# A local-attention convolution with whitening: first loads in smaller parts, one row point in other PSUM banks, one softmax later, half of the last products on quarters of the array

## The chip, the cores and the metric

The kernel runs on one core of a Trainium2 chip. The core has TensorE (PE, matrix products, with its weight loads shown as PEld), VectorE (DVE), ScalarE (ACT), GpSimd (POOL) and SyncE (SP), which each run their own queue of instructions in order, and 16 DMA engines. SP and POOL issue the DMAs. The metric is device microseconds of one execution; for the kernel before there are eight runs, and one execution that was profiled.

## The reference

What is computed, cut to what matters (B = 4 images, C = 256 channels, 64 x 64 pixels, 7 x 7 taps with dilation 2):

```python
k = conv(x, w1, 7x7, dilation 2, 256 -> 128 channels) + b1
k = conv(k, w2, 1x1, 128 -> 49) + b2
attn = softmax(k, axis=1)                       # 49 weights for each pixel
shifts = the 49 shifted copies of x (7 x 7, dilation 2)
y = einsum('bkchw,bkhw->bchw', shifts, attn)
# whitening of y, in 4 groups of 64 channels:
Sigma = 1e-5 * I + cov(y)                       # 64 x 64 for each group
P = five Newton steps to Sigma_N ** -0.5
out = (P * sqrt(1/trace)) @ (y - mean) * weight + bias
```

All data are fp32.

## The kernel before, in words

Rows and columns of an image are split by parity, since the dilation is 2. A "slot" holds the even or the odd rows of one image: 128 partitions (channels) x 2 halves of the channels (NCC = 2) x 32 rows x 64 columns. slots[2b + pr] is row parity pr of image b.

The two convolutions are first folded to one: at lines 181 to 226, w1 is loaded (four DMAs: the first 64 input channels of both halves, then the other 64), multiplied by w2 on PE in chunks of CB = 10 channels (line 210, into the two conv banks cv0 and cv1 in turn), evicted to tapT by ACT and DVE in turn, transposed in fours (line 228) and evicted to tap. Behind w1, the same SP queue loads slots 0 and 1 (load_x, line 129).

The 7 x 7 convolution is computed by a Toom-Cook scheme with seven points for rows and columns (EVAL, points 0, 1, -1, 2, -2, 1/2 and infinity). For a row point br, row_weights, weights, row_eval and col_eval make transformed weights wr and transformed images xh on DVE and ACT (helpers add, sub, madd at lines 289 to 296 record all of these); conv_bank (line 491) does the products for three banks of column points, BANKS = ((1, 2, 0), (3, 4, 6), (5,)), into cv0 and cv1 in turn; pv takes the result; col_interp and row_interp go back to logits. Points that are done directly in the column direction use direct (line 597): 56 passes of some 480 columns each. For image 0 the row points 4, 5 (the point 1/2), 0 and infinity are direct, and their sums go to acc, a PSUM tile of two banks, or to a conv bank. PE writes fp32 products in two passes, and the two row parities go to two column halves of the array (output partitions 0 to 48 and 64 to 112).

From line 690 or so to line 745 the order of image 0 is written out by hand (strict order on DVE): banks, row_weights, keep_weights, row_eval, direct0, col_interp, row_interp, prepare. The lines that the change touches are:

```python
    row_weights(5)
    keep_weights(5)
    col_interp(0, 2)
    ...
    row_eval(0, 5, [rb[0], rb[1], xrs[5]])
    direct0(4, 1)
    col_interp(0, 3)
```

For images 1 to 3 a loop over steps runs conv_step(k, i), i = 0, 1, 2 for the three banks of row point k. Between them a plan puts the softmax of the image before (soft(b, pc) for column parity pc: transposes at line 783, maxima on DVE at 789 and 792, exponentials on ACT at 797, normalisation on DVE at 801 to 810) and its gather: the weights go through zt (line 843), a DRAM buffer sd and 12 DMAs to band, which DVE transposes (line 894); PE turns x into blocks (912, evicted to xb at 920), sums with band (941, to y) and the result y is put back into the slot (960), turned again (973, 981) and added to the second moments sig (994). Image 1's steps begin with bank 0, bank 1, soft(0, 0), bank 2, the infinity product of the image (inf), soft(0, 1).

At the end the whitening matrices are made (whiten, lines 1172 to 1246; a generator for each half of the channels). Pm is 128 x 128 and block-diagonal with two 64 x 64 blocks. The last loop multiplies each 128 x 512 piece of the slots by Pm (line 1262), scales and shifts it on ACT (1273) or DVE (1277) in turn into a tile out (four buffers), and stores 512 KB for each pair of row parities (1281): 64 products, 32 stores.

Of the kernel before, what the change touches and what calls it, by code (L numbers as in the profile page):

```python
# [31 lines left out]
def kernel(  # L32
# [69 lines left out]
    def tp():  # L102
        return ps_tp.tile([P, 512], F32, tag="tp", name="tp")
# [74 lines left out]
    tapT = w1p.tile([P, KT, P], F32, name="tapT")  # L178


    for c0 in range(0, P, P // 2):
        for cc in range(NCC):
            nc.sync.dma_start(
                w1_sb[cc][:, c0 : c0 + P // 2].rearrange("o c t -> o (c t)"),
                w1[:, cc * P + c0 : cc * P + c0 + P // 2].rearrange("o c u v -> o (c u v)"),
            )
    load_x(0, 0, nc.sync)
    load_x(1, 1, nc.sync)
    for cc in range(NCC):
        cs = slice(cc * P, (cc + 1) * P)  # L190
        nc.sync.dma_start(gain_sb[:, cc : cc + 1], gain[0, cs].rearrange("c a b -> c (a b)"))
# [9 lines left out]
    def evict(k, o, i):  # L201
        (nc.vector.tensor_copy if k % 2 else nc.scalar.copy)(o, i)

    CB = 10
    for k, c0 in enumerate(range(0, P, CB)):
        n = min(CB, P - c0)
        t = cv_buf[k % 2]
# [463 lines left out]
    def direct0(br, sr):  # L671
        if br in kept:
            gb = gb5 if br == 5 else gbr
            direct(0, br, sr, acc[:, sr], [gb[:, v, :, sr] for v in range(KS)], xrs[br])
        else:
            u = KS - 1 - 4 * sr - (3 if br == INF else 0)
            w = [tap[:, UPOS[u], v] for v in range(KS)]
            direct(0, br, sr, conv_psum() if br == INF else acc[:, sr], w)
# [41 lines left out]
    bank(2, 2)  # L720
    row_weights(5)
    keep_weights(5)
    col_interp(0, 2)

    for sr in range(2):
        nc.scalar.copy(
# [4 lines left out]
        "p (q r c w) -> p q r c w", q=Q8, r=2, c=NCC  # L731
    )
    row_eval(0, 5, [rb[0], rb[1], xrs[5]])
    direct0(4, 1)
    col_interp(0, 3)
    row_interp(0, 0)
# [417 lines left out]
    nc.gpsimd.memset(blk, 0.0)  # L1154
    for g in range(P // GW):
# [10 lines left out]
    def square(name):  # L1166
        return bpool.tile([P, P], F32, tag="xb", name=name, bufs=4)

    wm, sc, beta = {}, {}, {}

    def whiten(cc):


        def evict(o, i):
            (nc.vector.tensor_copy if cc else nc.scalar.copy)(o, i)

        G = sig[:, cc]
        mu = work.tile([P, 1], F32, tag="mu", name=f"mu{cc}")
        nc.vector.tensor_scalar(mu, G[:, GW : GW + 1], 1.0 / NPIX, None, ALU.mult)
        D = square(f"D{cc}")  # L1180
        nc.vector.tensor_scalar(D, ident, mu, None, ALU.mult)
# [25 lines left out]


        i15 = square(f"i15_{cc}")
        nc.vector.tensor_scalar(i15, ident, 1.5, None, ALU.mult)  # L1210
        Pm = PS[:, 0]
        nc.vector.scalar_tensor_tensor(Pm, S, -0.5, i15, ALU.mult, ALU.add)
        yield

        for it in range(1, T_ITERS):
            t = tp()
            nc.tensor.matmul(
                t[:, : 2 * P], Pm, PS.rearrange("p a c -> p (a c)"), start=True, stop=True
            )
# [16 lines left out]
        scale = work.tile([P, 1], F32, tag="scale", name=f"scale{cc}")  # L1236
# [6 lines left out]
        bt = work.tile([P, 1], F32, tag="beta", name=f"beta{cc}")  # L1243
        nc.vector.tensor_scalar(bt, t[:, :1], scale, -1.0, ALU.mult, ALU.mult)
        nc.vector.tensor_tensor(bt, bt, shift_sb[:, cc : cc + 1], ALU.add)
        wm[cc], sc[cc], beta[cc] = Pm, scale, bt

    chains = [whiten(cc) for cc in range(NCC)]
    for _ in itertools.zip_longest(*chains):
        pass  # L1250


    NT = 512
    TR = NT // W
    n = 0
    for b in (3, 2, 1, 0):
        for cc in range(NCC):
            for q in range(SH // TR):
                st = rpool.tile([P, TR, 2, W], F32, tag="out", name=f"out_{b}_{cc}_{q}", bufs=4)
                for pr in range(2):  # L1260
                    t = tp()
                    nc.tensor.matmul(  # L1262
                        t,
                        wm[cc],
                        slots[2 * b + pr][:, cc, q * TR : (q + 1) * TR, :].rearrange(
                            "p r w -> p (r w)"
                        ),
                        start=True,
                        stop=True,
                    )  # L1270
                    t3 = t.rearrange("p (r w) -> p r w", w=W)
                    if n % 2 == 0:
                        nc.scalar.activation(  # L1273
                            st[:, :, pr, :], t3, AF.Identity, bias=beta[cc], scale=sc[cc]
                        )
                    else:
                        nc.vector.tensor_scalar(  # L1277
                            st[:, :, pr, :], t3, sc[cc], beta[cc], ALU.mult, ALU.add
                        )
                    n += 1  # L1280
                nc.sync.dma_start(
                    out[b, cc * P : (cc + 1) * P, 2 * q * TR : 2 * (q + 1) * TR, :],
                    st.rearrange("p r two w -> p (r two) w"),
                )


# [29 lines left out]
```

## Time and profile before

| | |
|---|---|
| median of 8 runs | 771.3 us (770.2 to 773.13) |
| the profiled execution | 770.2 us |
| its span, first to last instruction | 768.4 us |
| mean granted TensorE clock | 0.986 |

Busy time by stage, in us, from the windows of the profiled execution:

| stage | window | length | PE | DVE | ACT | DMA share |
|---|---|---|---|---|---|---|
| w1 folded, transposed | 0 to 33 | 33.0 | 21.8 | 11.6 | 8.1 | 0.98 |
| first direct products of image 0 | 33 to 58.3 | 25.3 | 23.5 | 24.4 | 6.0 | 0.85 |
| rest of image 0 | 58.3 to 172.1 | 113.8 | 105.5 | 106.4 | 30.7 | 0.15 |
| start of image 1, first softmax | 172.1 to 202.5 | 30.4 | 27.9 | 28.4 | 17.1 | 0.58 |
| images 1 to 3 with the gather of the one before | 202.5 to 604 | 401.5 | 385.1 | 368.8 | 197.8 | 0.43 |
| gather of the last image | 604 to 694 | 90.0 | 84.4 | 47.5 | 40.0 | 0.45 |
| whitening matrices | 694 to 708.5 | 14.5 | 11.3 | 10.4 | 2.6 | 0.01 |
| last products and stores | 708.5 to 768.4 | 59.9 | 55.2 | 26.3 | 24.9 | 0.69 |

How to read what follows: a line of the order of time gives start, duration, engine, line of the kernel, operation, the tile written and the tiles read, its shapes and how many instructions were merged; in square brackets stands how long the engine had been idle and which engine's result ended it. A line of the groups gives busy time in us and the mean of one instruction in ns behind the bar. A line of the windows gives for each engine the busy time and the number of instructions, then the granted clock, the DMA share and GB/s. An fp32 matmul shows as two passes. In the chain of work that ended last, PE has 40% of the span, DVE 33%, ACT 7%.

### The profile page before, as it was taken

The page shows a single profiled execution, that of the slowest core. Times are in us where ns is not written, and L with a number is a line of the kernel's source. Part 1 is how long each engine was busy: PE and PEld are TensorE (multiplying, and loading weights), DVE is VectorE, ACT ScalarE, POOL GpSimd, SP SyncE. Part 2 cuts the span into 40 slices and gives each one's busy share as a digit, 9 for nine tenths or more (in the row PEclk, how much of TensorE's full clock was granted, in tenths as well). Part 3 has the DMA queues.
Part 4 walks back from the last instruction along what each step waited for, and adds up shares of the span by engine and source line. Part 5 has one row for each costly group of instructions (what it writes and reads, how often), then busy time and mean ns, then how long its engine had stood idle before and what let it go on. Part 6 is the DMA issues. An engine that isn't in the chain of part 4 may idle for free.

```text
span 768.4 us, 18362 instructions
## 1 busy us (share of the span) xinstructions
PE 714.6 (93%) x7444; PEld 542.8 (71%) x7444; DVE 623.7 (81%) x1302; ACT 327.1 (43%) x950; POOL 34.2 (4%) x46
## 2 busy tenths in 40 slices
PE   4899997999999999989999999998999889998997
PEld 1349553265888886879988957898998678885443
DVE  2698999999999999979996999699979766535443
ACT  1413241035644653466445434725435663322443
POOL 0230000030000010001000100000000000000000
PEclk9999999899999999989999999999999999999999
DMA  8991110033554582055634820533422143380776
GB/s 332 241 303 62 44 74 37 0 139 124 161 164 146 193 297 68 21 192 186 226 113 167 287 68 2 165 102 107 162 71 85 44 144 115 106 326 25 288 307 280
DMA packets 58717, 114.76 MB, mean 149 GB/s; under 512 B 22615, under 2 KB 41736, under 8 KB 57352
## 3 DMA queue, kind: packets, MB, share of 16 engines
q1 hardware_dynamic: 54936, 94.71, 36.7%
q0 software_dynamic: 3696, 18.88, 7.3%
q8 instruction: 59, 0.97, 0.5%
q14 instruction: 26, 0.21, 0.1%
HBM read 66.23 MB, written 47.33 MB: 148 GB/s over the span
## 4 chain that ended last, share of the span: by engine, by line
PE 40%; DVE 33%; ACT 7%; issue 4%; DMA 3%; SPq 1%; DVEq 0%; ACTq 0%
PE y L941 12%; PE cv L491 12%; PE tp L1262 7%; DVE xh L296 4%; DVE pv L296 3%; PE tp L973 3%; PE tp L912 3%; PE sig L994 3%; DVE zz L296 3%; DVE band L894 2%; DVE ct L296 2%; DVE pv L292 2%; DVE ct L289 2%; ACT zt L843 2%; DVE rb L296 2%
## 5 line engine op out<-in xcount | busy, mean ns | idle before, releaser
L491 PE MATMUL cv<-xh,wr 128*49 128x128 f32 x4368 | 250.5, 275 | 0.0
L491 PEld LDWEIGHTS cv<-xh,wr 128*49 128x49 f32 x4368 | 244.2, 124 | 5.0 <-issue 2.5
L941 PE MATMUL y<-band,xb 128*128 128x224 f32 (+2 forms) x640 | 152.0, 377 | 12.0 <-ACT xb L920 10.3
L941 PEld LDWEIGHTS y<-band,xb 128*128 128x128 f32 x640 | 110.2, 194 | 33.6 <-ACT xb L920 12.8
L960 ACT ACTIVATE slot<-y,pivot 128x512 f32<-128x512 f32 x53 | 36.8, 741 | 60.5 <-PE y L941 60.5
L981 ACT COPY yt<-tp 128x256 f32<-128x256 f32 x128 | 45.5, 378 | 34.9 <-PE tp L973 33.8
L501 ACT COPY pv<-cv 113x486 f32<-113x486 f32 (+1 forms) x63 | 29.8, 475 | 68.4 <-PE cv L491 67.2
L912 PE MATMUL tp<-ident,slot 128*128 128x128 f32 x256 | 50.0, 297 | 7.4 <-ACT yt L981 7.4
L973 PE MATMUL tp<-ident,slot 128*128 128x128 f32 x256 | 51.8, 298 | 4.2 <-ACT xb L920 1.7
L894 DVE STREAM_TRANSPOSE band<-band 128x960 f32<-128x960 f32 (+1 forms) x48 | 51.0, 1063 | 2.8 <-DMA band<-sd 2.7
L973 PEld LDWEIGHTS tp<-ident,slot 128*128 128x128 f32 x256 | 41.3, 205 | 14.2 <-issue 4.5
L912 PEld LDWEIGHTS tp<-ident,slot 128*128 128x128 f32 x256 | 39.9, 205 | 14.3 <-ACT yt L981 9.3
L1277 DVE TENSOR_SCALAR out<-tp,scale,beta 128x512 f32<-128x512 f32 x32 | 25.9, 810 | 29.5 <-PE tp L1262 29.5
L843 ACT COPY zt<-d 32x112 f32<-32x112 f32 (+2 forms) x156 | 45.0, 288 | 1.7
L797 ACT ACTIVATE d<-tp,mx 128x49 f32<-128x49 f32 x128 | 37.0, 338 | 14.4 <-DVE mx L792 14.4
L1273 ACT ACTIVATE out<-tp,beta,scale 128x512 f32<-128x512 f32 x32 | 24.9, 778 | 32.0 <-PE tp L1262 32.0
L296 DVE SCALAR_TENSOR_TENSOR xh<-ct 128x512 f32<-128x512 f32 x42 | 28.0, 693 | 12.3 <-PE cv L491 12.1
L994 PEld LDWEIGHTS sig<-yt 128*64 128x64 f32 x1024 | 32.4, 137 | 6.3 <-issue 4.7
L994 PE MATMUL sig<-yt 128*64 128x65 f32 x1024 | 36.9, 225 | 0.0
L1262 PE MATMUL tp<-slot,PS 128*128 128x512 f32 x80 | 35.9, 593 | 0.0
L920 ACT COPY xb<-tp 128x256 f32<-128x256 f32 x87 | 30.5, 377 | 12.2 <-PE tp L912 11.5
L296 DVE SCALAR_TENSOR_TENSOR pv<-pv 113x162 f32<-113x162 f32 x105 | 34.3, 327 | 1.0
(203 smaller groups left out, 994.8 us busy)
## 6 DMA issues: line engine op xcount, KB each, us to landing
out_dram<-out SPq DMA_DIRECT2D x32, 512.0 KB, 2.6
sd<-zt SPq DMA_DIRECT2D x16, 896.0 KB, 3.9
slot<-in_x_dram POOLq DMA_DIRECT2D x12, 1024.0 KB, 9.4
band<-sd SPq DMA_DIRECT2D x128, 84.0 KB, 2.1
wr<-gd SPq DMA_DIRECT2D x15, 588.0 KB, 4.3
wr<-gd SPq DMA_DIRECT2D x15, 490.0 KB, 3.6
w<-in_L_conv_w_dram SPq DMA_DIRECT2D x4, 1568.0 KB, 11.9
spill<-slot POOLq DMA_DIRECT2D x3, 2048.0 KB, 7.5
```

What stands on the lines that cost most here:

```text
L296: return in_turn(STT(o, a, f, b, ALU.mult, ALU.add))
L491: nc.tensor.matmul(cv[h * HB : h * HB + KT, k, sr : sr + n, sc : sc + n], wv[:, sc, sr, cc], xh[bc][:, :n, h * NCC + cc, :n], start=(j == ...
L797: nc.scalar.activation(d[:, h, i], lt[i // NI][:, i % NI, h, :KT], AF.Exp, bias=mx[:, i, h : h + 1], accum_out=s[:, h, i : i + 1],)
L843: ins = nc.scalar.copy(o, i)
L894: nc.vector.transpose(f, f)
L912: nc.tensor.transpose(t[:, cc * P : (cc + 1) * P], xt[:, cc, CR * m : CR * (m + 1), bass.ds(pc, SW, 2)], ident,)
L941: nc.tensor.matmul(ps[:, cc, q0 - half * HALF : q1 - half * HALF, :], xb[:, cc * P : (cc + 1) * P], rhs, start=(k == 0), stop=(k == len(PI ...
L960: last = nc.scalar.activation(o, ps[:, cc], AF.Identity, bias=pivot[:, cc : cc + 1])
L973: nc.tensor.transpose(t[:, cc * P : (cc + 1) * P], yt[:, cc, CR * i : CR * (i + 1), bass.ds(pc, SW, 2)], ident,)
L981: nc.scalar.copy(yb.rearrange("p a g c -> p (a g) c")[:, :, :GW], t[:, :C].rearrange("p (e c) -> p e c", c=GW),)
L994: nc.tensor.matmul(sig[g * GW : (g + 1) * GW, cc], yb[:, cc, g, :GW], yb[:, cc, g], start=(count[0] == 0 and cc == 0), stop=(count[0] == 4 ...
L1262: nc.tensor.matmul(t, wm[cc], slots[2 * b + pr][:, cc, q * TR : (q + 1) * TR, :].rearrange("p r w -> p (r w)"), start=True, stop=True,)
```

## The change

Five edits in one:

- The load of w1 comes in five parts of 30, 30, 30, 20 and 18 input channels for both halves (ten DMAs instead of four). The parts end where the chunks of ten end.
- Slots 0 and 1 are loaded by row phases: the rows 4q + a of both slots and both halves for a = 3, then 0, 1, 2 (16 DMAs of 256 KB instead of four of 1 MB).
- The direct products of row point 5 (1/2) of image 0 go to the conv banks instead of acc, and row_eval(0, 5) stands before col_interp(0, 2).
- In image 1, soft(0, 0) stands behind the third bank's step instead of before it.
- In the last loop a group is two pieces of both row parities. The even rows are multiplied as before (two 128 x 128 products). The odd rows of the two pieces are multiplied by the two 64 x 64 blocks of Pm in four products, each on a quarter of the array: for the first piece, channels 0 to 63 go to output partitions 0 to 63 and 64 to 127 to 64 to 127; for the second piece the outputs are exchanged, so that the four products use the four pairs of row half and column half. They go to two PSUM banks, y's and the conv banks in turn. The exchanged piece is evicted in two instructions of 64 partitions, with scale and shift for the exchanged partitions, abx, which a product with an exchange matrix swap makes at the end of whiten. The tile out has six buffers.

```diff
-    for c0 in range(0, P, P // 2):
+    CB = 10
+    for c0, c1 in ((0, 3), (3, 6), (6, 9), (9, 11), (11, 13)):
+        c0, c1 = c0 * CB, min(c1 * CB, P)
         for cc in range(NCC):
             nc.sync.dma_start(
-                w1_sb[cc][:, c0 : c0 + P // 2].rearrange("o c t -> o (c t)"),
+                w1_sb[cc][:, c0:c1].rearrange("o c t -> o (c t)"),
...
-    load_x(0, 0, nc.sync)
-    load_x(1, 1, nc.sync)
+    for pr in range(2):
+        slots[pr] = store[pr]
+    for a in (3, 0, 1, 2):
+        for pr in range(2):
+            for cc in range(NCC):
+                nc.sync.dma_start(
+                    store[pr][:, cc].rearrange("c (q a) w -> c a q w", a=4)[:, a],
+                    x[0, cc * P : (cc + 1) * P].rearrange(
+                        "c (q a two) w -> c two a q w", two=2, a=4
+                    )[:, pr, a],
+                )
...
-            direct(0, br, sr, acc[:, sr], [gb[:, v, :, sr] for v in range(KS)], xrs[br])
+            direct(
+                0, br, sr, conv_psum() if br == 5 else acc[:, sr],
+                [gb[:, v, :, sr] for v in range(KS)], xrs[br],
+            )
...
-    col_interp(0, 2)
...
     row_eval(0, 5, [rb[0], rb[1], xrs[5]])
+    col_interp(0, 2)
     direct0(4, 1)
...
-                *steps[:2], (0, lambda: soft(0, 0)), steps[2], inf, (0, lambda: soft(0, 1)),
+                *steps[:3], (0, lambda: soft(0, 0)), inf, (0, lambda: soft(0, 1)),
...
+    swap = rpool.tile([P, P], F32, name="swap")
+    for g in range(P // GW):
+        nc.gpsimd.tensor_copy(
+            swap[:, g * GW : (g + 1) * GW], ident[:, (1 - g) * GW : (2 - g) * GW]
+        )
...
+        t = tp()
+        nc.tensor.matmul(t[:, :2], swap, ab, start=True, stop=True)
+        abx[cc] = work.tile([P, 2], F32, tag="abx", name=f"abx{cc}")
+        nc.vector.tensor_copy(abx[cc], t[:, :2])
...
+                def plain(k):
+                    t = tp()
+                    pe(nc.tensor.matmul(t, wm[cc], y[0][k], start=True, stop=True))
+                    out_rows(st[k][:, :, 0, :], rows_of(t), sc[cc], beta[cc])
...
+                plain(0)
+                for k in range(2):
+                    for i in (G0, G1):
+                        o = i if k == 0 else (G1 if i is G0 else G0)
+                        pe(
+                            nc.tensor.matmul(
+                                ts[k][o], wm[cc][i, i], y[1][k][i],
+                                start=True, stop=True, skip_group_check=True,
+                            )
+                        )
+                out_rows(st[0][:, :, 1, :], rows_of(ts[0]), sc[cc], beta[cc])
+                store(0)
+                for i, o in ((G1, G0), (G0, G1)):
+                    out_rows(
+                        st[1][o][:, :, 1, :], rows_of(ts[1])[i], abx[cc][i, 0:1], abx[cc][i, 1:2]
+                    )
+                plain(1)
+                store(1)
```

out_rows is the scaling and shifting on ACT and DVE in turn; store is the DMA of 512 KB.

More of the change, by code (lines that the diff above doesn't have):

```diff
@@ L178 @@
     tapT = w1p.tile([P, KT, P], F32, name="tapT")
-    for c0 in range(0, P, P // 2):
+    CB = 10
+    for c0, c1 in ((0, 3), (3, 6), (6, 9), (9, 11), (11, 13)):
+        c0, c1 = c0 * CB, min(c1 * CB, P)
         for cc in range(NCC):
             nc.sync.dma_start(
-                w1_sb[cc][:, c0 : c0 + P // 2].rearrange("o c t -> o (c t)"),
-                w1[:, cc * P + c0 : cc * P + c0 + P // 2].rearrange("o c u v -> o (c u v)"),
-            )
-    load_x(0, 0, nc.sync)
-    load_x(1, 1, nc.sync)
+                w1_sb[cc][:, c0:c1].rearrange("o c t -> o (c t)"),
+                w1[:, cc * P + c0 : cc * P + c1].rearrange("o c u v -> o (c u v)"),
+            )
+    for pr in range(2):
[9 more added lines that the diff above has]
+                )
     for cc in range(NCC):
@@ L202, in evict @@
         (nc.vector.tensor_copy if k % 2 else nc.scalar.copy)(o, i)
-    CB = 10
     for k, c0 in enumerate(range(0, P, CB)):
@@ L1167, in square @@
         return bpool.tile([P, P], F32, tag="xb", name=name, bufs=4)
-    wm, sc, beta = {}, {}, {}
+    wm, sc, beta, abx = {}, {}, {}, {}
     def whiten(cc):
@@ L1235, in whiten @@
         nc.vector.scalar_tensor_tensor(q, qi, rtr, q, ALU.mult, ALU.add)
-        scale = work.tile([P, 1], F32, tag="scale", name=f"scale{cc}")
+        ab = work.tile([P, 2], F32, tag="ab", name=f"ab{cc}")
+        scale = ab[:, 0:1]
         nc.vector.scalar_tensor_tensor(
@@ L1242, in whiten @@
         yield
-        bt = work.tile([P, 1], F32, tag="beta", name=f"beta{cc}")
+        bt = ab[:, 1:2]
         nc.vector.tensor_scalar(bt, t[:, :1], scale, -1.0, ALU.mult, ALU.mult)
@@ L1246, in whiten @@
         wm[cc], sc[cc], beta[cc] = Pm, scale, bt
+        yield
+        t = tp()
+        nc.tensor.matmul(t[:, :2], swap, ab, start=True, stop=True)
+        abx[cc] = work.tile([P, 2], F32, tag="abx", name=f"abx{cc}")
+        nc.vector.tensor_copy(abx[cc], t[:, :2])
     chains = [whiten(cc) for cc in range(NCC)]
@@ L1254, with out_rows, two_banks @@
     TR = NT // W
-    n = 0
+    n = [0]
+    def out_rows(o, i, scale, bias):
+        n[0] += 1
+        if n[0] % 2:
+            nc.scalar.activation(o, i, AF.Identity, bias=bias, scale=scale)
+        else:
+            nc.vector.tensor_scalar(o, i, scale, bias, ALU.mult, ALU.add)
+    def two_banks():
+        while True:
+            t = ps_y.tile([P, 2, NT], F32, tag="y", name="apply")
+            yield [t[:, k] for k in range(2)]
+            yield cv_buf
+    G0, G1 = slice(0, GW), slice(GW, P)
@@ L1256 @@
+    two = two_banks()
     for b in (3, 2, 1, 0):
         for cc in range(NCC):
-            for q in range(SH // TR):
-                st = rpool.tile([P, TR, 2, W], F32, tag="out", name=f"out_{b}_{cc}_{q}", bufs=4)
-                for pr in range(2):
-                    t = tp()
[L1262 to L1269, printed above, removed]
-                    )
[L1271 to L1274, printed above, removed]
-                        )
[L1276 to L1284, printed above, removed]
@@ new lines, with store @@
+            for q in range(0, SH // TR, 2):
+                st = [
+                    rpool.tile([P, TR, 2, W], F32, tag="out", name=f"out_{b}_{cc}_{q + k}", bufs=6)
+                    for k in range(2)
+                ]
+                y = [
+                    [
+                        slots[2 * b + pr][:, cc, (q + k) * TR : (q + k + 1) * TR, :].rearrange(
+                            "p r w -> p (r w)"
+                        )
+                        for k in range(2)
+                    ]
+                    for pr in range(2)
+                ]
+                rows_of = lambda t: t.rearrange("p (r w) -> p r w", w=W)
+                ts = next(two)
+                def plain(k):
+                    t = tp()
+                    pe(nc.tensor.matmul(t, wm[cc], y[0][k], start=True, stop=True))
+                    out_rows(st[k][:, :, 0, :], rows_of(t), sc[cc], beta[cc])
+                def store(k):
+                    nc.sync.dma_start(
+                        out[
+                            b, cc * P : (cc + 1) * P, 2 * (q + k) * TR : 2 * (q + k + 1) * TR, :
+                        ],
+                        st[k].rearrange("p r two w -> p (r two) w"),
+                    )
+                plain(0)
[7 more added lines that the diff above has]
+                            )
+                        )
+                out_rows(st[0][:, :, 1, :], rows_of(ts[0]), sc[cc], beta[cc])
[6 more added lines that the diff above has]
+                store(1)
```

## The prediction

> **What bounds the kernel now.** I read the share of busy time first, then the busy time by stage, then the order of time at the places that the change touches, and last the instruction order of both programs, engine by engine. From the page:
>
> ```profile
> PE 714.6 (93%) x7444; PEld 542.8 (71%) x7444; DVE 623.7 (81%) x1302; ACT 327.1 (43%) x950; POOL 34.2 (4%) x46
> L1262 PE MATMUL tp<-slot,PS 128*128 128x512 f32 x80 | 35.9, 593 | 0.0
> L994 PE MATMUL sig<-yt 128*64 128x65 f32 x1024 | 36.9, 225 | 0.0
> ```
>
> The kernel is a chain of stages with different limits, so three places are read on their own. First the head, 0 to 66 us, in order of time:
>
> ```profile
> 9.26 1.87 PE L210 MATMUL cv<-w,w2T 128*49 128x490 f32 x2 [4.54 <-DMA w<-in_L_conv_w_dram]
> 13.03 13.54 PE L210 MATMUL cv<-w,w2T 128*49 128x490 f32 x50 [1.90 <-DMA w<-in_L_conv_w_dram]
> 36.75 9.94 PE L597 MATMUL cv<-slot,tap 128*49 128x512 f32 x48 [1.84 <-DMA slot<-in_x_dram]
> 42.32 4.62 DVE L289 TENSOR_TENSOR rb<-slot 128x1024 f32<-128x1024 f32 x4
> 64.28 0.36 DVE L289 TENSOR_TENSOR wr<-ct 128x196 f32<-128x196 f32 x1 [3.14 <-PE cv L491]
> ```
>
> PE folds w1 only from 13.03, when 64 columns of both halves have landed; it meets the last x load at 36.75; and VectorE, without a gap from 29.66, waits once, for PE's first bank, until 64.28. From there to 172 VectorE is the engine without idle time (106.4 of 113.8 us busy) and the chain of waits runs along it. Second, the turn from image 0 to image 1:
>
> ```profile
> 134.76 14.21 PE L597 MATMUL acc<-slot,gb 128*49 128x512 f32 x56 [4.77 <-DVE zz L289]
> 177.76 0.30 ACT L501 COPY pv<-cv 113x162 f32<-113x162 f32 x1 [4.84 <-PE cv L491]
> 177.96 0.31 ACT L797 ACTIVATE d<-tp,mx 128x49 f32<-128x49 f32 x1
> 202.54 1.34 PE L941 MATMUL y<-band,xb 128*128 128x320 f32 x4 [1.65 <-ACT xb L920]
> ```
>
> PE waits for VectorE at 134.76, but VectorE does not wait for PE there. Third, the tail:
>
> ```profile
> 708.49 27.71 PE L1262 MATMUL tp<-slot,PS 128*128 128x512 f32 x64
> 740.00:750.00 10.00, 10.00 (x25) 4.46 (x24) 4.56 (x7) 4.67 (x6) 0.00 (x0) 1.00 0.74 302
> ```
>
> 128 passes (two for each of 64 fp32 products) stand 0.429 us apart, 55 us without a gap, while ACT and DVE are 46% busy and DMA has a share of 0.74 at 302 GB/s. The tail is PE's alone.
>
> **What the Trainium skill says.** (1) "TensorEngine Tiling (Array Packing)", section Tiling Modes: a 64x64 configuration has four independent tiles, and a change of tiling mode drains TensorE. The trace shows two column halves side by side (line 994: 32 passes of 65 columns in 1.15 us, 36 ns each, where 65 columns alone take 65 x 0.429/512 = 54 ns), never row halves; its drain, from records on both sides of such a change (lines 941 to 994 and 994 to 912), is 0.10 us each way. (2) "TensorE: Matmul & The Clock Gate", Part 3, says of packed tiles that matmuls are "strict FIFO, no reordering". The trace disagrees: at 13.03 two passes for different column halves start 7 ns apart although the first one's second pass stands between them in the program. (3) The same page, Part 1: after an idle window of some 3.4 us PE runs at half rate. The trace agrees: after 4.77 us of idle the 56 passes at 134.76 took 14.21 us, against 11.59 when warm. (4) "DMA: Bandwidth & Descriptors", Specifications, gives about 358 GB/s per core for HBM. The w1 load moved 398 to 452 GB/s, so I take the measured packet: 4096 B in 159 ns, 16 engines, 412 GB/s.
>
> **The change part by part.**
>
> *w1 in five parts.* The same bytes flow: a 12,544 B packet takes 469 ns, and the first half-load (8 packets per engine, 3.75 us) landed at 9.26, so the stream starts at 5.45. Between the two measured packets, a 5,880 B packet should take 224 ns, so both halves of the first 30 columns land at 5.45 + 2 x 8 x 0.224 = 9.1 us, against 13.03. Later parts land at 12.7, 16.3, 18.8 and 21.0; chunks 3, 6, 9 and 11 would want them at 13.4, 16.2, 19.2 and 21.0 if the old rhythm is moved by 3.9. They just fit. The last part of tapT moves from 27.1 to about 23.3: 3.8 us earlier for PE and VectorE. Six more issues on SP at about 0.4 us run ahead of the stream and cost nothing.
>
> *x by row phases.* Still 256 B packets, 4 MB in about 16.3 us (20.4 to 36.7), now four quarters, near 25, 29, 33 and 37 us. The INF product needs only phase 3 and the next only phase 0. Transposes of the weights end at 33.0 - 3.8 = 29.2, so PE no longer meets x: 112 passes at 0.203 us end near 52.1 where they ended at 58.3. PE gains 6 us, of which 2.1 is the stall. VectorE reaches its first use of all phases at 42.3 - 3.8 = 38.5, with x due at 37.3; slots 2 and 3 (POOL's queue, from about 36) collide with the last quarter for up to 1 us. VectorE's wait for the first bank shrinks from 3.14 to about 1 us, so from 64 on it is 3.8 + 2.1 = 5.9 us ahead. A miss of 1 us in x is absorbed by that remaining wait. Taken: -5.9; bounds -3 (slower 256 B reads) and -6.5.
>
> *Row point 1/2.* Both products go to the two conv banks, and row_eval(0, 5) (8.2 us on DVE) comes before col_interp(0, 2) (6.8 us). DVE has the same work in another order, and no wait of its own to lose, so it gains nothing. PE does the two products from 129.9 to 153 instead of 134.8 to 161.2. A new wait comes in: bank 2 of image 1's first point shares cv1 with the second product, and DVE reads that only at 167.8. On PE the third bank and the softmax transposes queue behind it, until about 175.9 on the old clock; DVE comes to those only at 178, so it is covered. Cost 0.
>
> *First softmax behind the third bank.* In the new DVE order the maxima stand behind all four adds of the next row point and their negation behind the 2,048-element add. So: pivot 1.13, four adds 4.7, maxima 0.95, sum 2.2 after 172.09 gives 181.3, and the exponentials start at 181.9 instead of 177.96. zt is filled from 186.9 instead of 183.7 and sd leaves 3.2 us later. On the other side PE does the INF product of image 1 before, DVE loses its waits of 1.27 and 0.73 us, and the first gather matmul was not waiting for the band but for ACT, which was held by col_interp of the first point (copy at 201.44). In the new order I get that copy at 198.2, xb at 201.5 and the first y near 201.6 against 202.54. Sum -0.5, bounds -2.5 and +3.5 (the whole delay of the exponentials arrives). After 260 the orders are the same, so what is gained is carried on.
>
> *Whitening products.* A group is two chunks of both row parities. Before: 8 passes, 8 x 0.429 = 3.43 us. After: 4 plain passes 1.72, four 64x64 products with two passes each, side by side, 2 x 0.429 + 0.02 = 0.88, two mode changes 0.20: 2.80 us. 16 groups: 44.8 for 54.9, -10.1. Evictions are five a group, 5 x 0.8 / 2 = 2.0 us on each engine, under 2.8. Stores are 1.05 MB a group, 2.54 us at 412 GB/s: under 2.8, but 91%. Added before: beta must be complete, then a 128x2 product with swap for each half: first main product at about 709.4 instead of 708.5, +0.9. Two stores now leave close together at the end, +0.4. The tail: -8.8. Its unknown is the four-way overlap; bounds: nothing overlaps more than two (4 passes long, 58.2 us, so +3.3 + 1.3 = +4.6), and full overlap, -9.5. The page (1) and the freedom between the two halves in the trace make me take four. swap's two copies on POOL lie near 601 where POOL is idle.
>
> **The sum.** -5.9 - 0.5 - 8.8 = -15.2 on the profiled span of 768.4 (execution 770.2): 753.2 and 755.0. The runs' median is 771.3, 1.1 above this execution; so 756.1.
>
> **Rivals.**
> - *Two at a time.* If row halves of the array do not run side by side, the four products take four pass times: -6.4 + 4.6 gives 769.5. For it: no row half was ever seen here. Against: the skill's four tiles, and the queues per half seen at 13.03. If three run at once, about 763.
> - *Slower: one tile blocks the queue.* Each fp32 product has two passes on the same tile. If PE begins passes strictly in program order where row halves are involved, each second pass holds the next product back: starts at 0, 1, 1, 2, 2, 3, 3, 4 pass times, so 5 in all. A group then takes 9 passes and 0.2 us: 4.06 x 16 = 65.0, +10.1 + 1.3, less 6.4: 776. It decides from 1.83 us for the four products on (1.72 - 0.20 + 5.05/16), where I expect 0.88. Against it stands the start at 13.03.
> - *The stores become the bound.* At 358 GB/s the 16.8 MB need 46.9 us from the first store at 712: about 758. It only shaves my forecast.
> - *The change does not do what it says at the head*: strided reads make x late and VectorE waits at its row evaluation; then 3 us of the 5.9 are left and the time is 759.
>
> **Chances.** Forecast, with the full stores beside it, 0.76; x late 0.06; two or three at a time 0.11; blocked queue or another loss 0.07. The forecast's own range is 751 to 761; it leaves too much out, so I take 750 to 766, which adds late x and three at once. What a measurement of this kernel can tell from no change is about 0.2%, 1.5 us: two at a time sits on this edge and is split. Faster 0.87, within 0.05, slower 0.08.
>
> **What would show it.** First w1 product with both halves near 9.1; line 597 without a wait on x; DVE's wait for the first bank near 1 us instead of 3.14; the two gb products from about 124 on; exponentials later against the pivot (10 us after it, now 6) yet the first y no later; in the tail a group each 2.8 us, with four passes starting within 30 ns, DMA share about 0.9. A group of 3.6 or 4.1 us proves me wrong, as does a VectorE that waits for x before row_eval by more than 2 us.

## The result, and the profile after

The kernel after took 760.38 us in the median of 11 runs (756.73 to 763.39); the kernel before, in 32 runs beside it and earlier, 772.2 us (768.9 to 774.99). The ratio is 0.985, with a 95% interval of 0.9833 to 0.9867. A second series on another chip gave 761.72 us beside 771.07, ratio 0.9886 (0.9858 to 0.9914). So the change saves 9 to 12 us; 15.2 were forecast. The profiled execution of the kernel after took 763.28 us, its span is 761.5 (before: 768.4).

The busy time, from the page of the kernel after:

```profile
PE 708.4 (93%) x7512; PEld 534.6 (70%) x7512; DVE 630.6 (83%) x1312; ACT 332.4 (44%) x958; POOL 34.4 (5%) x48
```

The shares have hardly moved. The three places have to be read on their own again. The head of the kernel after, in order of time:

```profile
6.87 15.62 PE L221 MATMUL cv<-w,w2T 128*49 128x490 f32 x52 [2.15 <-DMA w<-in_L_conv_w_dram]
...
28.90 11.59 PE L608 MATMUL cv<-slot,tap 128*49 128x512 f32 x56
40.31 11.55 PE L608 MATMUL acc<-slot,tap 128*49 128x512 f32 x56
...
38.22 4.62 DVE L300 TENSOR_TENSOR rb<-slot 128x1024 f32<-128x1024 f32 x4
57.29 0.36 DVE L300 TENSOR_TENSOR wr<-ct 128x196 f32<-128x196 f32 x1 [0.43 <-PE cv L502]
```

PE starts on w1 at 6.87 and does not wait for it again, the direct passes (line 597 before, 608 now) run without a wait for x, and VectorE's wait for the first bank has shrunk from 3.14 to 0.43 us: at this point the kernel is 6.99 us ahead (57.29 for 64.28). VectorE's first instruction behind image 0 (pivot, 165.08 for 172.09) has the same lead. Then the turn to image 1:

```profile
151.35 6.96 PE L502 MATMUL cv<-xh,wr 128*49 128x128 f32 x96 [5.59 <-DVE xh L300]
161.54 7.93 PE L502 MATMUL cv<-xh,wr 128*49 128x128 f32 x112 [3.23 <-DVE zz L300]
169.40 1.22 PE L797 MATMUL tp<-ident,slot 113*128 113x113 f32 x8
...
174.08 0.68 ACT L468 COPY xh<-rb 128x512 f32<-128x512 f32 x1 [4.28 <-DVE rb L300]
174.65 0.31 ACT L811 ACTIVATE d<-tp,mx 128x49 f32<-128x49 f32 x1
...
195.74 1.18 DVE L908 STREAM_TRANSPOSE band<-band 128x960 f32<-128x960 f32 x1 [3.36 <-DMA band<-sd]
197.02 1.31 PE L955 MATMUL y<-band,xb 128*128 128x320 f32 x4 [3.12 <-DMA band<-sd]
```

PE waits twice for VectorE, the softmax transposes come at 169.40, the exponentials start 9.6 us behind the pivot (5.9 before), and now both VectorE and PE wait for the bands. The first y is 5.5 us earlier than before, not 7, and when the whitening matrices begin (the first matmul with blk, 691.98 for 694.87) only 2.9 us of the lead are left. Two single profiles can mislead by some us (a second profile of the old head follows with the tail experiment), but the runs below show that part of the gain was lost here. The tail, in order of time, and two windows of it (busy us and count of PE, PEld, DVE, ACT, POOL, then the granted clock, the DMA share, GB/s):

```profile
706.63 1.40 PE L1324 MATMUL tp<-slot,PS 128*128 128x512 f32 x2
707.96 1.99 PE L1340 MATMUL apply<-slot,PS 64*64 64x512 f32 x8
709.88 2.39 PE L1324 MATMUL tp<-slot,PS 128*128 128x512 f32 x4
...
715.13 1.09 PE L1340 MATMUL apply<-slot,PS 64*64 64x512 f32 x8
716.15 1.98 PE L1324 MATMUL tp<-slot,PS 128*128 128x512 f32 x4
718.07 1.09 PE L1340 MATMUL cv<-slot,PS 64*64 64x512 f32 x8
```

```profile
708.00:710.00 2.00, 2.00 (x10) 0.39 (x9) 0.00 (x0) 0.78 (x1) 0.00 (x0) 0.50 0.00 0
...
734.00:744.00 10.00, 10.00 (x40) 3.08 (x39) 7.04 (x9) 6.27 (x9) 0.00 (x0) 1.00 0.89 365
```

The four products on quarters run side by side: in the trace their second passes start at 715.612, 715.619, 715.625 and 715.632. A group takes 2.93 us (715.13 to 718.07). But the first products stand in a stretch at half clock (707.3 to 710.7), and from the first main product to the end it is 54.9 us where it was 59.9.

### The profile page after: what moved, and what is told of

Its sections match the earlier page's. It is cut to its first block, busy times and chain, and to the rows that moved or that the text cites. A ratio compares the mean times of both kernels' runs of the same rounds, so it can differ in the third digit from the quotient of the medians.

```text
span 761.5 us, 18542 instructions
## 1 busy us (share of the span) xinstructions
PE 708.4 (93%) x7512; PEld 534.6 (70%) x7512; DVE 630.6 (83%) x1312; ACT 332.4 (44%) x958; POOL 34.4 (5%) x48
## 4 chain that ended last, share of the span: by engine, by line
DVE 37%; PE 36%; ACT 7%; issue 4%; DMA 4%; SPq 0%; DVEq 0%; ACTq 0%
PE y L955 11%; PE cv L502 9%; PE tp L1324 4%; DVE xh L307 4%; DVE pv L307 3%; DVE zz L307 3%; PE tp L926 3%; PE sig L1008 3%; PE tp L987 2%; DVE rb L307 2%; DVE ct L300 2%; ACT zt L857 2%; DVE ct L307 2%; DMA band<-sd 2%; DVE rb L300 2%
## 5 line engine op out<-in xcount | busy, mean ns | idle before, releaser
L955 PE MATMUL y<-band,xb 128*128 128x224 f32 (+2 forms) x640 | 153.7, 380 | 13.5 <-ACT xb L934 8.7
L307 DVE SCALAR_TENSOR_TENSOR xh<-ct 128x512 f32<-128x512 f32 x42 | 27.9, 686 | 12.3 <-PE cv L502 12.1
L934 DVE COPY xb<-tp 128x256 f32<-128x256 f32 x41 | 16.5, 422 | 22.2 <-PE tp L926 22.2
L608 PE MATMUL cv<-slot,wi 128*49 128x496 f32 (+3 forms) x168 | 34.8, 571 | 0.0
L811 ACT ACTIVATION_READ_ACCUMULATOR d<-tp,mx 128x1 f32 x128 | 30.8, 243 | 0.0
```

The lines of the kernel that those rows point to most:

```text
L307: return in_turn(STT(o, a, f, b, ALU.mult, ALU.add))
L811: nc.scalar.activation(d[:, h, i], lt[i // NI][:, i % NI, h, :KT], AF.Exp, bias=mx[:, i, h : h + 1], accum_out=s[:, h, i : i + 1],)
L934: (nc.vector.tensor_copy if tail else nc.scalar.copy)(xb, t[:, :C])
L955: nc.tensor.matmul(ps[:, cc, q0 - half * HALF : q1 - half * HALF, :], xb[:, cc * P : (cc + 1) * P], rhs, start=(k == 0), stop=(k == len(PI ...
```

## The experiments

Each was run in 5 rounds beside the kernel before; the short diffs leave out what is not needed to see the edit.

### The parts alone: head, w1 without x, tail

The kernel before with the two edits of the loads only.

> The kernel before with only the new loads (w1 in five parts, x by row phases). Theory A (the head's gain is real and is lost later only because the first softmax stands behind the third bank): VectorE's first bank wait ends near 57.3 as in the changed kernel, 7.0 us earlier than before, and at 260 us the lead is still 6 to 7 us: time about 765, -7. Theory B (the turn to image 1 loses it whatever the order of the softmax, since band, x load and blocks do not come earlier by as much): the lead at 260 us is about 3 us, time about 769. My prediction's term was -5.9: 766.

It took 765.11 us beside 771.64, ratio 0.9913 (0.9889 to 0.9938). VectorE's first bank wait ends at 57.19, and the whitening begins at 687.88, 7.0 us before that of the first profile of the kernel before. Theory B, which left a gain of about 2.5 us, is out; the head does not lose its gain by itself. Now w1 in five parts, with x as before:

```diff
+    for c0, c1 in ((0, 3), (3, 6), (6, 9), (9, 11), (11, 13)):
...
     load_x(0, 0, nc.sync)
     load_x(1, 1, nc.sync)
```

> The kernel before with w1 in five parts alone, x loaded as before. By my steps: the last tapT 3.8 us earlier, but PE still meets the last x load near 36.7, so that the direct passes gain nothing but what PE does before the stall: VectorE's first bank wait ends at most 0 to 1 us earlier, time 770 to 771. Rival: VectorE, not PE, carries the gain from the w1 parts, and x arrives earlier as the stream starts earlier: then up to -4, 767.

It took 773.96 us beside 771.15, ratio 1.0031 (1.0016 to 1.0046): a little slower, which neither side expected. Its head in order of time:

```profile
33.81 1.95 PE L599 MATMUL cv<-slot,tap 128*49 128x512 f32 x4 [3.99 <-DMA slot<-in_x_dram]
37.47 11.31 PE L599 MATMUL cv<-slot,tap 128*49 128x512 f32 x48 [1.71 <-DMA slot<-in_x_dram]
...
66.38 0.36 DVE L291 TENSOR_TENSOR wr<-ct 128x196 f32<-128x196 f32 x1 [9.65 <-PE cv L493]
```

PE reaches the direct passes 4.2 us earlier (28.77) and meets x twice; the last x load ends at 37.47, later than before (36.75), and the 48 passes behind it take 11.31 us, not 9.94, since TensorE's clock is halved from 33.4 to 40.3 after the first wait. Why the last x load is late was not tested; the trace shows that POOL's queue begins to load slots 2 and 3 at 34.0 here and at 38.2 before, so that they share the DMA engines with it. The parts of w1 are worth nothing, and less, until x comes in the order in which it is used.

The kernel before with the new last loop only:

> The kernel before with only the new last loop and what it needs (swap, abx). Prediction's term: -8.8, so 763.4, a group 2.80 us. By the trace of the changed kernel: a group 2.93 us (two mode changes cost 0.36 us, not 0.20), and the stretch from the first main product to the end 54.9 for 59.9 with one half-rate window of 3.4 us at its start; so -5 to -6: about 766.5, and -7 where the half-rate window does not fall on the start.

It took 765.89 us beside 771.64, ratio 0.9926 (0.9901 to 0.9951): -5.75, not -8.8. First main product to the end: 55.0 us, and a group again takes 2.93. Up to the whitening this kernel is the kernel before, so its trace is a second profile of the old head:

```profile
62.64 0.36 DVE L289 TENSOR_TENSOR wr<-ct 128x196 f32<-128x196 f32 x1 [1.07 <-PE cv L491]
```

Here PE waited 0.5 us for x in all, VectorE's first bank wait ended at 62.64 and not at 64.28, and the whitening began at 691.64 and not at 694.87. The old head is not the same in every execution, while in the eleven profiles with the new one this wait ends between 57.12 and 57.38. So a lead read from two profiles is no better than 1.6 us at the head and 3.2 us at the whitening; the times of many executions are firmer.

### The middle: which edit gives the lead back

The changed kernel, with the softmax put back in front of the third bank, and with the edit of row point 1/2 undone:

```diff
-                *steps[:3], (0, lambda: soft(0, 0)), inf, (0, lambda: soft(0, 1)),
+                *steps[:2], (0, lambda: soft(0, 0)), steps[2], inf, (0, lambda: soft(0, 1)),
```

> The changed kernel with the first softmax of image 1 back in front of the third bank; all else as changed. Theory A (the moved softmax makes the weights' way to DRAM late by 3 us against the lead, and puts the 12 band loads behind the 1 MB x load): faster than the changed kernel by 2 to 4 us, about 757; first y near 195.6 (202.5 less 7) instead of 197.0, and the 3.4 us wait of VectorE for band gone. Theory B (my prediction's term of -0.5, loss has another cause): slower than the changed kernel by 0 to 1, about 761.

```diff
-                0, br, sr, conv_psum() if br == 5 else acc[:, sr],
+            direct(0, br, sr, acc[:, sr], [gb[:, v, :, sr] for v in range(KS)], xrs[br])
...
+    col_interp(0, 2)
...
     row_eval(0, 5, [rb[0], rb[1], xrs[5]])
-    col_interp(0, 2)
```

> The changed kernel with row point 1/2 of image 0 back in acc and its row evaluation back behind the column interpolation. My prediction's term is 0: the time of the changed kernel, about 760.4, since VectorE sets the pace there and does the same work. Rival: the earlier products on PE are what lets the third bank and the softmax transposes come in time, then it is slower than the changed kernel by 1 to 3 us, 761.5 to 763.5.

The first took 763.54 us, ratio 0.9879 (0.9854 to 0.9904), no faster than the changed kernel (0.985 and 0.9886): the theory that the later softmax costs 2 to 4 us fell. The second took 758.3, ratio 0.9832 (0.9808 to 0.9857). That is lower than the changed kernel, which neither of its theories had, but the interval overlaps that of the changed kernel's first series (from 0.9833) and ends just below that of the second (from 0.9858). So the row point is the suspect, and the experiments that follow have to decide. The kernel without that edit, in order of time:

```profile
127.80 12.99 PE L608 MATMUL acc<-slot,gb 128*49 128x512 f32 x56 [4.76 <-DVE zz L300]
...
152.88 11.76 PE L502 MATMUL cv<-xh,wr 128*49 128x128 f32 x208
166.01 1.21 PE L794 MATMUL tp<-ident,slot 113*128 113x113 f32 x8 [1.37 <-ACT slot L590]
...
169.78 0.30 ACT L808 ACTIVATE d<-tp,mx 128x49 f32<-128x49 f32 x1 [3.64 <-issue]
...
192.44 1.32 PE L952 MATMUL y<-band,xb 128*128 128x320 f32 x4 [1.93 <-DMA band<-sd]
```

With acc, PE's wait (4.76 us) stands in front of a product that nobody is waiting for, and all three banks of image 1 follow in one piece (208 passes, the transposes at 166.01). With the conv banks PE does that product early, and its idle time moves to where it hurts: 5.59 us in front of the first bank, for xh that VectorE makes no earlier, and 3.23 us in front of the second, which needs the PSUM bank that VectorE's add reads at 160.8 (the recorded expectations speak of the third bank; it is the second that waits, and the third queues behind it). The transposes come 3.4 us later. A part of that is TensorE's clock: half-rate stretches lie on these products, behind the waits (151.0 to 154.4 and 161.2 to 164.6), and the 112 passes behind the second wait take 7.93 us where they take 6.48 in a later profile without such a stretch there. With acc the half-rate stretch falls on the product that nobody is waiting for.

The order of VectorE's work has changed too, far from the edit. First without it, then with it (the lines of VectorE in the fastest version with the edit, the last run below):

```profile
166.25 1.21 DVE L300 TENSOR_TENSOR rb<-slot 128x1024 f32<-128x1024 f32 x1
167.38 1.03 DVE L800 TENSOR_REDUCE mx<-tp 128x8 f32<-128x392 f32 x2
```

```profile
167.90 1.21 PE L797 MATMUL tp<-ident,slot 113*128 113x113 f32 x8
167.37 3.49 DVE L300 TENSOR_TENSOR rb<-slot 128x1024 f32<-128x1024 f32 x3
170.78 1.03 DVE L803 TENSOR_REDUCE mx<-tp 128x8 f32<-128x392 f32 x2
```

The maxima stood behind one add of the next row point; now they stand behind four, on an engine that has no gap there, and ScalarE has a copy in front of the exponentials. These start at 174.65 instead of 169.78, and the first y is 4.6 us later. That the order does this, and not how late the transposes come, shows in the second view: there no half-rate stretch lies on the second bank, the transposes come at 167.90 and not at 169.40, and the maxima (170.78 for 170.82) and exponentials (174.62 for 174.65) are no earlier. Two halves of the edit were taken apart.

```diff
     keep_weights(5)
+    col_interp(0, 2)
...
     row_eval(0, 5, [rb[0], rb[1], xrs[5]])
-    col_interp(0, 2)
```

> The changed kernel with the row evaluation of point 1/2 back behind the column interpolation, but its direct products still in the conv banks. Theory C (sharing the conv banks with image 1's third bank makes that bank, and with it the softmax transposes and ScalarE's order, late): as the changed kernel, 760 to 761, the transposes of the first softmax end near 170.6 and not 167.2, and ScalarE's copy of xh stands in front of the exponentials. Rival D (the new place of the row evaluation does it): as without the whole edit, 758.

762.37 us beside 771.07, ratio 0.9885 (0.9861 to 0.9909): like the changed kernel in its series (0.9886), transposes at 169.46, the maxima behind four adds and the exponentials at 174.70. The shared banks do it, not the place of row_eval. A run with the shared banks and VectorE's old order was not made. Then ScalarE's order alone:

```diff
+        for o, x in late:
+            tc.add_manual_dep(nc.scalar.copy(o, x).ins, exps[-1].ins.name, ...)
```

> The changed kernel with one difference in ScalarE's order alone: the two copies of xh for the next row point (0.68 and 0.77 us) stand behind the 16 exponentials of the first softmax, not one in front and one behind. Theory C': the exponentials waited 4.28 us behind a copy that waits for VectorE; they now start at about 172.2 (transposes 170.6, maxima, negation) instead of 174.65, and the first y comes 2 us earlier, near 195; time 758.5 to 759.5. Rival: the bands then still wait for the 1 MB x load and the time stays at 760.4, or PE's first gather is held by ScalarE's xb instead.

761.13 us, ratio 0.9867 (0.984 to 0.9893), which can't be told from the changed kernel. The exponentials started at 174.14, only 0.5 us earlier, waiting 4.23 us for VectorE's maxima; the first y stayed at 196.98. So the copy in front of them is not what holds them: the maxima behind four adds on VectorE do.

Where the softmax is in its old place, the shared banks seem to cost about as much (see the account below), but later: the first y of that run comes at 195.54, with the full lead, and ScalarE's order takes it back at 216, where the copy of xh that waits for VectorE stands in front of the copies for which PE waits (order of time):

```profile
216.11 0.66 ACT L468 COPY xh<-rb 128x512 f32<-128x512 f32 x1 [3.79 <-DVE rb L307]
216.67 0.56 ACT L512 COPY pv<-cv 113x486 f32<-113x486 f32 x1
217.13 0.65 ACT L995 COPY yt<-tp 128x256 f32<-128x256 f32 x2
...
217.56 0.50 PE L926 MATMUL tp<-ident,slot 128*128 128x128 f32 x2 [2.64 <-ACT yt L995]
```

### The changed kernel once more, and the tail taken further

> The changed kernel once more, on the chip of the others of this call, to compare with them: about 0.985 of the time before. Theory E (free half-rate windows of TensorE's clock make the profiled span differ from run to run by 1 to 2 us for each window of 3.4 us on the path): another span than 761.5, and other places of the windows; the first y near 197.0 and the group of 2.93 us in the tail come again.

Its time is in the first section: 0.9886. Its profiled span was 759.5, its first y at 196.94, its group 2.93 us. Of its half-rate stretches one lies at 196.2 for 6.8 us, where the first profile has one at 219.2 for 3.4; the others lie within 3 us of those of the first profile. So the stretches move in part, as Theory E has it; what one of them costs this run does not show.

Since PE sets the pace of the tail, all products were put on quarters, on top of the kernel without the row point edit:

```diff
-                plain(0)
...
-                                ts[k][o], wm[cc][i, i], y[1][k][i],
+                                ts[k][o], wm[cc][i, i], y[k][i],
...
-                plain(1)
...
+            yield [tp(), tp()]
```

> The changed kernel with row point 1/2 undone, and in the last loop all products on quarters of the array: even rows straight, odd rows exchanged, four 64x64 products for each 512 KB store, three evictions for it instead of two and a half, no plain products and so no mode change, three pairs of PSUM banks. Theory F: PE needs 32 x (2 x 0.429 + 0.05) = 29 us and is no bound any more; evictions 96 x 0.8 / 2 = 38 us on each engine; the stores 16.8 MB at 412 GB/s 40.7 us, at the 367 GB/s seen in the changed kernel 45.7 us. The tail from the first product to the end 44 to 49 us instead of 54.9, time 749 to 753. Rival G: without mode changes the quarters do not run four at a time (their weights are loaded behind each other), PE stays the bound, no gain: 758.

763.88 us beside 771.07, ratio 0.9907 (0.9883 to 0.9931), slower than the mixed loop. The waits of its tail (from 710 to 750: engine and line, whom it waited for, us in total, times, longest), and a window of it:

```profile
ACT out L1288 <- DVE out L1290: 11.0, 12, 0.9
DVE out L1290 <- ACT out L1288: 9.9, 12, 0.9
```

```profile
720.00:730.00 10.00, 7.18 (x50) 2.06 (x48) 7.29 (x9) 6.99 (x10) 0.00 (x0) 1.00 0.78 315
```

Rival G, that PE stays the bound, is wrong too: PE starts groups of four 0.91 us apart and is idle over a quarter of the time. ScalarE and VectorE wait for each other, 0.9 us at a time: two evictions into the same tile out, by different engines, run one after the other, though they write different rows or partitions. So one engine for each store:

```diff
     def out_rows(o, i, scale, bias):
-        n[0] += 1
...
                 ts = next(two)
+                n[0] += 1
```

> The run with all products on quarters, with one difference: the three evictions of a store are done by one engine, ScalarE and VectorE in turn from store to store. Theory H (evictions of one out tile wait for each other across the engines, ScalarE 0.92 us for VectorE and back, so that a store takes 1.65 us): a store then costs 3 x 0.8 / 2 = 1.2 us on the evictions, 1.29 us of DMA at 408 GB/s, 0.91 us of PE; 32 x 1.3 = 42 us, the tail 47 instead of 59.8 us, time 750 to 752. Rival: PE's waits come from the three pairs of banks, or the stores run at 315 GB/s for another reason; then the time stays near 763.

753.29 us beside 771.15, ratio 0.9769 (0.9744 to 0.9795). First main product to the end: 48.8 us instead of 59.8. The same window:

```profile
720.00:730.00 10.00, 8.21 (x66) 2.86 (x70) 9.72 (x12) 9.38 (x13) 0.00 (x0) 1.00 1.02 417
```

Now the DMA engines are full, and VectorE (9.72 us of 10) and ScalarE (9.38) nearly so. Last, the product with swap behind the first four products:

> As the run with one engine for each store, and the products with swap stand behind the first four 64x64 products instead of in front of them. Theory I: PE's small products and waits between the last Newton step and the first main product (0.38 us of idle time and 0.6 us of work) are gone from the path, 0.8 us, and with them the half-rate window of 3.4 us that stands at the start of the tail in every profile with swap and in none without (1.7 us where PE sets the pace, less where the evictions do): 0.8 to 2 us faster than that run. Rival: the window depends on where the free windows fall; then 0 to 0.8 us.

751.97 us, ratio 0.9744 (0.9716 to 0.9771), faster than both kernels of this study. The intervals of this run and the one before it overlap, so that the 1.3 us between them are not certain. The trace shows what changed: from the first matmul with blk to the first main product it is 13.8 us and not 14.7, and no half-rate stretch stands at the tail's start.

The row point was then put into this fastest version again, as a check on what it costs:

> The fastest version so far (head, later softmax, all products on quarters with one engine for each store, late swap) with the edit of row point 1/2 put in again; it had 0.9744 of the time before without it. Theory C: the third bank of image 1 waits for VectorE's add near 161.4, exponentials start near 174.6 instead of 169.7, the first y near 197.0 instead of 191.7, the whitening starts 3 to 5 us later than the 685.4 to 688.4 of the runs without the edit; ratio 0.979 to 0.981. Rival: the difference seen so far is the scatter of the half-rate windows; then the whitening starts inside 685.4 to 688.4 and the ratio stays at 0.974 to 0.976.

756.05 us beside 772.22, ratio 0.9791 (0.9778 to 0.9804): 3.6 us slower by the ratios, on another chip, with intervals that just do not touch. The exponentials start at 174.62, the first y at 195.67 (forecast near 197.0), the whitening at 689.1. Between the two profiles of the fastest version the first y is 4.0 us later with the row point and the whitening 3.7, so the loss is there when the first y comes and is carried on. All profiles side by side, in us:

| profile | 1/2 in conv banks | exponentials | first y | first matmul with blk |
|---|---|---|---|---|
| before | no | 177.96 | 202.54 | 694.87 |
| tail only (old head) | no | 176.26 | 201.33 | 691.64 |
| w1 in five parts only | no | 179.56 | 205.35 | 697.49 |
| head only | no | 170.56 | 195.75 | 687.88 |
| without row point (four kernels, by tail) | no | 169.57 to 169.78 | 191.61 to 192.44 | 685.37 to 688.41 |
| softmax back | yes | 171.81 | 195.54 | 691.92 |
| changed kernel, twice | yes | 174.65, 174.52 | 197.02, 196.94 | 691.98, 689.92 |
| banks only | yes | 174.70 | 197.01 | 691.80 |
| copies late | yes | 174.14 | 196.98 | 687.71 |
| row point in the fastest | yes | 174.62 | 195.67 | 689.10 |

With the later softmax the whitening begins at 686.6 in the mean of the four kernels without the shared banks, and at 690.1 in the mean of the five profiles with them. The two groups overlap (688.41 and 687.71), and those with the shared banks also have more half-rate time before the whitening (13.7 to 20.5 us between 100 and 680 us, beside 6.8 to 10.2), so that a single profile does not give the cost.

## Why the prediction was right, and where not

*Head.* Right in mechanism: -5.9 forecast, -6.5 in time alone, and a lead of 5.3 to 7.0 us, depending on which profile of the old head it is taken from. Against the first one, the transposes end at 28.90 for 32.99 (4.1, forecast 3.8), the stall on x is gone (1.84), and 1.07 us come from passes no longer out of step: before, the wait for x put the two column halves' passes out of pairs at 46.46 and 57.84. VectorE's wait is 0.43 where 1 was forecast, and x was in time at 38.22. What the prediction did not see is that the w1 parts alone would lose 2 us.

*Row point 1/2: the step that failed.* "Cost 0". The new wait was foreseen in its place. Its length was half of what came: PE was to be queued until 168.9 on the new clock, 1.7 us later than without the edit, and the transposes end at 170.6, 3.4 later (2.0 later in the last run, where the second bank ran at full clock). What failed was its cover: "DVE comes to those only at 178, so it is covered". That late place of the maxima was itself a result of the shared banks: with the softmax in its new place the maxima stand behind one add without them and behind four with them. That the planner (what sets the order of instructions when the kernel is built) puts work where it expects its inputs is my reading of these two orders, not tested. I read the new order, blamed the softmax's move for the late maxima, and used their lateness to excuse the wait. Measured: 3.6 us in the fastest version. Without the later softmax it is 4.2 us by the medians (-8.1 against the sum of head and tail, -6.53 and -5.75) or 3.1 by the ratios; with three intervals of 1.9 us in it, this difference alone would not prove the loss.

*First softmax behind the third bank.* -0.5 forecast. Without the row point the changed kernel gains 13.3 us where head and tail together gain 12.3, so about -1; the difference is smaller than these intervals, and the term is not confirmed. The working behind the -0.5 was wrong: without the shared banks the exponentials start 4.7 us behind the pivot, not 10.

*Whitening products.* -8.8 forecast, -5.75 measured: what the sum put in for costs was too small. The unknown, whether four run side by side, came out as taken: the Trainium skill, "TensorEngine Tiling (Array Packing)", Tiling Modes, says four independent tiles, and the starts 7 ns apart agree. Two mode changes cost 0.36 us for each group (2.93 less six pass times), not 0.20: about 0.09 and 0.11 at the changes themselves, and 0.05 and 0.10 because the second pass behind each change comes later than one pass time. In the trace the weights of that pass are loaded only after the change, and it starts 0.43 us after that load starts, which fits but was not tested. A group is 0.13 us longer than forecast, 2.1 us in 16. The first group ran at half clock (1.7 us). The end grew by 1.3 us instead of 0.4: the last evictions of the exchanged piece wait for each other and two stores go out behind them. The start was +1.0 in this profile for +0.9, and the other profiles with swap in front have up to +2.1.

*The sum.* Head -6.5, row point +3.1 to +4.2, softmax -1, tail -5.75: -9.1 to -10.2, beside the measured -9.4 and -11.8. That the time still lies in the stated range of 750 to 766 us is owed to the width of the range: two of four terms were off by 3 us or more, both to the same side. The rivals "two at a time", "blocked queue" and "x late" did not come in; the stores became a bound only once the quarters were used throughout, and then at 390 to 417 GB/s, not at 358.

## What to carry to other kernels

Before a new wait is called covered, ask whether the thing that covers it would be there without the wait: where a planner sets the order of the engines, as here, moving a product to another buffer can move other engines' work too, and a move to a shared PSUM bank has to be priced with the queue behind it. Two load edits may be worth something only together, so price each one alone for what it meets next. When packing makes TensorE fast, look at once at what is behind it: here evictions of one tile by two engines ran one after the other, and giving each store to one engine was worth 10.6 us.

## What the runs showed of the hardware

TensorE's half-rate stretches explain much of the scatter. The Trainium skill, "TensorE: Matmul & The Clock Gate", Part 1, says that the activity window is free-running, so that the same kernel differs from run to run. The traces agree: all stretches inside the kernels are 3.4 or 6.8 us long, and over the 12 executions of the changed kernel's first series the span goes from 755.0 us at a mean clock of 0.989 to 761.6 at 0.976. It is not the whole of the scatter: in the second series one execution took 764.5 us at 0.980.

Some stretches are not chance: in all nine profiles with the swap product in front of the tail a stretch of 3.4 us begins between 0.3 us before and 0.9 us behind the first main product; in the five without it, none does. PE need not be idle for that. In the 3.41 us before this stretch PE was busy for 2.82 or 2.83 us in each of the nine; in the last such windows before the main products of the other five it was busy for 3.2 us or more. No run was made to find where the limit lies.

The stores ran at 390 to 417 GB/s (windows of 10 us between 710 and 740 in the three runs with one engine for each store), with the 16 DMA engines full or nearly so. That is above the 358 GB/s that "DMA: Bandwidth & Descriptors", Specifications, in the Trainium skill gives for each core and works out as half of a memory stack that two cores share; this kernel runs on one core, and for it the measurement decides.
